# Three PSUM buffers for the exps of a scan kernel, products with C one scan later, and sums over states in bursts in a shared PSUM bank

## The chip, the core and the metric

The kernel runs on one core of one Trainium2 chip. The core has TensorE (PE, matrix products), VectorE (DVE), ScalarE (ACT, activation functions), GpSimd (POOL) and SyncE (SP, which here issues nearly all transfers). They run at once, each through its own queue in order, and wait for one another by semaphores. Matrix products land in PSUM, which has eight banks of 512 float32 columns on 128 partitions; everything else lies in SBUF. The metric is the device time of one execution in microseconds, the lower the better.

## The reference

Eight images of 56 x 56 pixels with 192 channels go through four layers: three state-space layers (the first with a convolution branch beside it) and one window-attention layer with an MLP. All is float32. The change touches the core of the state-space layers, the selective scan. For each of 4 directions k over the 3,136 pixels, each of 192 channels d and each of 16 states n:

```python
def step(h, t):
    u_t, d_t, b_t, c_t = t
    h = exp(d_t[..., None] * A) * h + (d_t * u_t)[..., None] * b_t[:, :, None, :]
    return (h, einsum('bkdn,bkn->bkd', h, c_t))
ys = scan(step, 0, (xs4, delta, Bs, Cs)) + Ds * xs4      # and a sum over the directions
```

Directions 0 and 2 run over rows forwards and backwards, 1 and 3 over columns. Delta is the softplus of a small projection; B and C are other rows of the same projection.

## The kernel before, in words

**Tiling.** A chunk is 784 pixels (CK), four per direction. A unit is one layer of one image, one direction and one chunk: 8 images x 3 layers x 4 x 4 = 384 units. A unit has two halves h of 96 channels. A half has 12 steps: three channel groups j of 32 channels times four state groups sg of 4 states. A tile of 128 partitions holds 32 channels x 4 states. That makes 9,216 steps; `run` writes them out in one order, and all engines follow it.

**A step.** In `make`, ScalarE computes exp(delta x A) from `dsp` (delta spread over four states, by a transfer) into a PSUM buffer `ps_x` of two banks, and GpSimd computes `db = usp x bt` (delta x u, spread likewise, times a row of B spread over 32 channels). VectorE then runs the scan over the 784 columns, in place in `ps_x`, with the last state of the chunk before as its start. It multiplies the result with `ct` (the row of C) into `hc`. Every fourth step the scan writes to `hc` and GpSimd does that product. ScalarE copies the scan's last column to `state` (all but the last chunk). TensorE multiplies `hc` with `esum`, a 128 x 32 matrix of ones and zeros, which adds the four states up, and accumulates in PSUM.

**The order in `run`, before.** At step s: the state copy of step s-2, then the exp and db of step s, then scan and product of step s-1 on VectorE, GpSimd's product of step s-2 if it has one, and the sums of three products (j = 0, 1, 2) up to step s-4. Within a half, sg is the outer loop and j the inner one. The sums of a half lie in a buffer of their own, `ps_y` (two banks), which begins with a product of the identity (or of D) with what is accumulated so far; at its end one copy (`merge`) of 96 x 784 brings it back to `act`. PSUM holds two buffers `ps_x` (four banks), `ps_y` (two) and two single banks `ps_p` for all other work.

**Other work.** Projections, softplus, layer norms, convolutions and attention of neighbouring images run beside the scans. They are Python generators in three queues (`ahead`, `urgent`, `back`). At the end of each step the loop lets them issue pieces while a budget for TensorE and ScalarE (SPARE, MOST, unchanged) lasts. `yield 1` puts a piece off to the next step; LAG = 1 is the distance between a matmul and what reads its bank. A piece takes a bank by `bank` or `all_banks` and gives it back with `free`. Functions that need another activation table (softplus, silu, gelu) run in steps that `table_time` allows: step modulo 4 equal to 1 or 2.

**Transfers.** `prepare` computes delta and du for the next half and issues their spreads (2,304 of `dsp`, 2,304 of `usp`); `load_bc` issues the rows of B and C for the next unit (1,536 each). All stand in SP's queue in the order of the program, each waiting there for its buffer.

The functions that the change touches, as they were before:

Of the kernel before, what the change touches and what calls it, by code (L numbers as in the profile page):

```python
# [36 lines left out]
HW = 56  # L37
# [7 lines left out]
N = 16  # L45
# [93 lines left out]
class Net:  # L139
    def __init__(self, ctx, tc, a, out):  # L140
# [19 lines left out]
        self.psum = ctx.enter_context(tc.tile_pool(name="psum", bufs=2, space=bass.MemoryType.PSUM))  # L160
        self.psum1 = ctx.enter_context(tc.tile_pool(name="psum1", bufs=1, space=bass.MemoryType.PSUM))
        for n in (1, 2, 4):
            setattr(self, f"s{n}", ctx.enter_context(tc.tile_pool(name=f"s{n}", bufs=n)))
        self.s6 = ctx.enter_context(tc.tile_pool(name="s6", bufs=HCS))
# [12 lines left out]
    def ps(self, tag, p=128, n=512):  # L177
        if tag == "y":
            t = self.psum1.tile([128, 1024], F32, name="ps_y")
        elif tag == "p":  # L180
            t = self.banks[0]
            self.banks.rotate()
        else:
            t = self.psum.tile([128, 1024], F32, name=f"ps_{tag}", tag=tag)
        return t[:p, :n]
# [185 lines left out]
    def bank(self, spare=0):  # L371


        (p,) = yield from self.all_banks(1, spare)
        return p

    def all_banks(self, n, spare=0):
        rank = self.rank
        while len(self.banks) < n + spare or any(at >= self.now - 1 for at in self.asked[rank + 1 :]):
            self.asked[rank] = self.now  # L380
            yield 1
        self.asked[rank] = -9
        return [self.banks.popleft() for _ in range(n)]

# [8 lines left out]
    def table_time(self):  # L393


        while self.step % 4 not in (1, 2) and not self.forced:
            yield 1
# [9 lines left out]
    def together(self, width, works):  # L407
# [3 lines left out]
        while works or tasks:  # L411
# [10 lines left out]
            else:  # L422
                yield 1
# [4 lines left out]
    def ln_cm(self, x, n, sq):  # L428
# [10 lines left out]
        yield 1  # L439
        yield from self.to_norm(x, n, sq)  # L440

    def to_norm(self, x, n, sq):
# [3 lines left out]
        yield 1  # L446
# [11 lines left out]
        yield 1  # L458
# [41 lines left out]
    def ssm_front(self, b):  # L500
# [3 lines left out]
        with tc.tile_pool(name="f1", bufs=1) as f1, tc.tile_pool(name="f2", bufs=2) as f2:  # L504
# [14 lines left out]
            def depthwise(r, c, u):  # L519
# [13 lines left out]
                yield 1  # L533

            def gate(xnt, r, e, sz):
# [12 lines left out]
                yield 1  # L548
# [3 lines left out]
            for r in range(NR + 1):  # L552
                sz = u = None
                if r < NR:
# [15 lines left out]
                    yield 1  # L570
# [3 lines left out]
                    yield 1  # L574
# [10 lines left out]
                    yield 1  # L585
# [7 lines left out]
                yield 1  # L593
# [8 lines left out]
    def conv_front(self, b):  # L602
# [3 lines left out]
        with tc.tile_pool(name="f1", bufs=1) as f1, tc.tile_pool(name="f2", bufs=2) as f2:  # L606
# [20 lines left out]
            def first(r):  # L627
# [15 lines left out]
                yield 1  # L643

            def second(r):
# [7 lines left out]
                yield 1  # L653

            def third(r):
# [6 lines left out]
                yield 1  # L662
# [3 lines left out]
                def last(c):  # L666
# [6 lines left out]
                    yield 1  # L673
# [10 lines left out]
                    yield 1  # L684
# [35 lines left out]
    def after_half(self, g, q):  # L720
# [6 lines left out]
        if l == 2:  # L727
            w = aux.rearrange("p c (a b) -> p c a b", b=HW)
            for c in range(2):
# [5 lines left out]
                yield 1  # L735
# [6 lines left out]
        yield 1  # L742
        if l == 0:
# [6 lines left out]
            ps = yield from self.all_banks(2)  # L750
            for c in range(2):
                for j in range(2):
                    nc.tensor.matmul(
                        ps[c][:CH, :HC], self.wout[:, j, CH * c : CH * c + CH], y[:, j, :],
# [775 lines left out]
```

## Time and profile before

| What | Value |
|---|---|
| Median of three runs | 27,059.5 us (27,051.76 to 27,069.66) |
| Span of the profiled execution, first to last instruction | 27,058.8 us; the page gives no other time of that execution |
| Instructions | 260,255 |
| Busy: TensorE, VectorE, ScalarE, GpSimd | 68%, 89%, 64%, 85% of the span |
| Granted TensorE clock, mean | 0.756 |
| DMA engines busy in the main queue | 56.0%; 128 GB/s |
| Scans, 128 x 784 | 9,216 of 1.78 to 1.85 us each |
| Products with C on VectorE, on GpSimd | 6,912 of 0.975 us, 2,304 of 1.847 us |
| Products db on GpSimd | 9,216 of 1.857 us |
| Exps on ScalarE | 9,216 of 0.919 us |

A group line of the profile names engine, operation, output and inputs by the program's names, shapes and count; behind the first bar stand the busy time in us and the mean of one in ns; behind the second the idle time of that engine just before these instructions, with what ended most of it. Nearly all instructions are recorded under one line of the program (L109, a helper), so groups are told apart by names and shapes. In a list of waits the numbers are us in total, how often, and the longest. In a timeline the first numbers are start and duration in us.

### The profile page before, as it was taken

What the parts mean: (1) busy time and instruction counts of PE and PEld (TensorE: products, weight loads), DVE (VectorE), ACT (ScalarE), POOL (GpSimd) and SP (SyncE); (2) the same over time, 40 slices, a digit from 0 to 9 for tenths busy, and PEclk for the clock granted to TensorE, in tenths of its full rate; (3) what the DMA queues carried; (4) which work ended last, traced back from release to release, by engine and by line L of the source; (5) the groups of instructions that cost most, each with busy time, mean ns of one, the idle gap of its engine ahead of it and who ended that gap; (6) DMA issues with size and microseconds to landing.
All of it is one profiled execution on the core that took longest, in us unless ns stands there. A gap on an engine that the chain in (4) does not pass through costs nothing. (4 is left out here: it accounts for less than half of the span.)

```text
span 27058.8 us, 260255 instructions
## 1 busy us (share of the span) xinstructions
PE 18495.3 (68%) x76788; PEld 6432.0 (24%) x76788; DVE 24122.4 (89%) x18972; ACT 17211.8 (64%) x30893; POOL 23054.4 (85%) x13199
## 2 busy tenths in 40 slices
PE   6675567676676666766667676677766776676657
PEld 2221122222222222222222222222212222222114
DVE  5999999999999899999999999989999899999991
ACT  4655566665666666666666666666666666666655
POOL 5888988888888888888888888888888888888991
PEclk7776677777777777777777777777777777777777
DMA  4555565556555565555655556555565555555550
GB/s 96 135 138 124 133 136 133 126 127 139 135 132 127 125 144 132 132 126 129 142 131 132 127 131 140 133 129 127 131 140 131 129 128 135 134 129 129 130 132 25
DMA packets 1503447, 3472.21 MB, mean 128 GB/s; under 512 B 310618, under 2 KB 503219, under 8 KB 1502020
## 3 DMA queue, kind: packets, MB, share of 16 engines
q1 hardware_dynamic: 1496452, 3455.15, 56.0%
q8 instruction: 606, 9.93, 0.1%
q0 software_dynamic: 3072, 0.31, 0.1%
q14 instruction: 821, 6.73, 0.1%
q10 hardware_dynamic: 2496, 0.09, 0.0%
HBM read 1457.23 MB, written 147.89 MB: 59 GB/s over the span
## 5 line engine op out<-in xcount | busy, mean ns | idle before, releaser
L109 POOL TENSOR_TENSOR db<-usp,bt 128x784 f32<-128x784 f32 x9216 | 16832.7, 1857 | 161.8 <-DMA usp<-du 129.3
L109 DVE TENSOR_TENSOR_SCAN ps_x<-ps_x,state,db 128x784 f32<-128x784 f32 x5184 | 9569.7, 1846 | 834.0 <-ACT state L109 358.7
L109 ACT ACTIVATE ps_x<-dsp,A 128x784 f32<-128x784 f32 x9216 | 8464.1, 919 | 2496.9 <-DVE hc L109 2190.5
L109 PE MATMUL ps_y<-hc,esum 128*32 128x392 f32 x36864 | 6959.3, 641 | 1147.3 <-POOL hc L109 780.6
L109 DVE TENSOR_TENSOR hc<-ps_x,ct 128x784 f32<-128x784 f32 x6912 | 6739.5, 975 | 651.4 <-DVE ps_x L109 11.0
L109 POOL TENSOR_TENSOR hc<-hc,ct 128x784 f32<-128x784 f32 x2304 | 4254.4, 1847 | 2696.2 <-ACT state L109 2104.5
L109 ACT COPY state<-ps_x 128x1 f32<-128x1 f32 x5184 | 831.4, 160 | 4659.5 <-DVE hc L109 4637.4
L109 DVE TENSOR_TENSOR_SCAN hc<-ps_x,state,db 128x784 f32<-128x784 f32 x1728 | 3181.7, 1841 | 161.6 <-POOL db L109 58.2
L109 DVE TENSOR_TENSOR_SCAN ps_x<-ps_x,db 128x784 f32<-128x784 f32 x1728 | 3085.0, 1785 | 261.1 <-ACT state L109 149.1
L109 PEld LDWEIGHTS ps_y<-hc,esum 128*32 128x32 f32 x36864 | 1630.6, 130 | 6096.7 <-issue 3212.3
L109 PE MATMUL ps_y<-act,ident 96*96 96x392 f32 x2304 | 1612.2, 835 | 1760.4 <-ACT act L109 1746.4
L109 PE MATMUL ps_p<-act,act 13*96 13x392 f32 (+1 forms) x3072 | 1513.0, 605 | 1116.6 <-ACT s L109 210.4
L109 POOL TENSOR_TENSOR du<-delta,act 96x784 f32<-96x784 f32 x768 | 1567.9, 2042 | 201.3 <-ACT delta L109 198.7
L109 PE MATMUL ps_p<-act,wx 96*88 96x392 f32 (+1 forms) x1536 | 985.8, 778 | 686.9 <-ACT delta L109 394.0
L109 ACT ACT_TABLE_LOAD x896 | 1149.6, 1283 | 34.4 <-PE ps_p L109 18.9
L390 ACT ACT_TABLE_LOAD x897 | 1150.9, 1283 | 15.6
L109 PEld LDWEIGHTS ps_y<-act,ident 96*96 96x96 f32 x2304 | 465.0, 223 | 2603.1 <-ACT act L109 2056.6
L109 DVE TENSOR_TENSOR_SCAN hc<-ps_x,db 128x784 f32<-128x784 f32 x576 | 1025.8, 1781 | 58.8 <-ACT state L109 38.0
L109 PEld LDWEIGHTS ps_p<-act,act 13*96 13x96 f32 (+1 forms) x3072 | 465.4, 180 | 2033.6 <-issue 373.5
L109 ACT COPY act<-ps_y 96x784 f32<-96x784 f32 x768 | 928.0, 1208 | 8.5 <-PE ps_y L109 8.5
L109 PE MATMUL ps_p<-xip,diag 96*96 96x448 f32 x2016 | 864.0, 580 | 94.4 <-ACT delta L109 94.3
L109 ACT COPY state<-hc 128x1 f32<-128x1 f32 x1728 | 328.6, 190 | 883.6 <-DVE hc L109 880.4
(212 smaller groups left out, 18126.0 us busy)
## 6 DMA issues: line engine op xcount, KB each, us to landing
dsp<-delta SPq DMA_DIRECT2D x2304, 392.0 KB
usp<-du SPq DMA_DIRECT2D x2304, 392.0 KB
bt<-bcd SPq DMA_DIRECT2D x1536, 392.0 KB
ct<-bcd SPq DMA_DIRECT2D x1536, 392.0 KB
wf<-in_wf SPq DMA_DIRECT2D x128, 288.0 KB
wf<-wf2d SPq DMA_DIRECT2D x128, 288.0 KB
bcd<-bcx SPq DMA_DIRECT2D x256, 134.8 KB
szd<-sz SPq DMA_DIRECT2D x56, 336.0 KB
```

The lines of the kernel that those rows point to most:

```text
L109: return call(out, *args, **k)
L390: self.tc.nc.scalar.preload_act_table_set(LN_EXP)
```

## The change

**PSUM.** `ps_x` has three buffers (six banks). `ps_y` is gone: the sums use one of the two single banks. The buffers in SBUF become rings of their own (RINGS): three `dsp` and `usp` in place of four, five `bt`, six `ct`, four `db`, seven `hc` in place of eight.

**Steps.** Within a half, j is now the outer loop and sg the inner one, so four steps in a row share `dsp` and `usp` and make up one group of 32 channels. At step s VectorE gets the scan of step s-1 and then the product of step s-2. The step whose product GpSimd makes is sg = 1 (AWAY), and it is issued at s-3.

**Sums.** A group's four products are added up in two bursts, the first at the end of the group's sixth step (`begin_sum`, then sg 0 and 2), the second one step later (sg 1 and 3), with the merge in that same step. The 784 columns are cut into three parts of 280, 280 and 224 (PARTS), which go to three 32-partition parts of one bank. The merge is three copies of 32 partitions per group, nine per half. `bank_now` takes the bank for it and lets waiting pieces run until one is free; `kept` makes other work leave one over.

**Other work.** It runs twice a step: once behind the exp and db and ahead of the scan, and once behind the product. Many `yield 1` become `yield NEAR` (0.5). Table switches come at step modulo 4 equal to 0, at most one task a step; `prepare` takes both banks only at step modulo 4 equal to 3.

**Transfers.** The spreads are put in a list (`later`) and issued nine steps before the group that uses them. The rows of B and C are loaded by `load_rows`, at four late steps of a unit, B one step ahead of C.

The core of the diff:

```diff
-        self.psum = ...tile_pool(name="psum", bufs=2, space=PSUM)
-        self.psum1 = ...tile_pool(name="psum1", bufs=1, space=PSUM)
+        self.psum = ...tile_pool(name="psum", bufs=3, space=PSUM)
...
     def table_time(self):
-        while self.step % 4 not in (1, 2) and not self.forced:
-            yield 1
+        while (self.step % SN or self.switched == self.step) and not self.forced:
+            yield NEAR
+        self.switched = self.step
...
             if s < S:
                 made[s] = self.make(*steps[s])
+            while self.later and self.later[0][0] <= s:
+                self.spread_rows(*self.later.popleft()[1:])
+            self.near = True
+            self.pieces(left)
             t = s - 1
             if 0 <= t < S:
-                U, h, sg, j = steps[t]
+                U, h, j, sg = steps[t]
                 x, db = made[t]
-                pool = t % 4 == 3
-                hc = self.s6.tile([128, CK], F32, name="hc")
-                hs = hc if pool else x
+                hs = x
+                if sg == AWAY:
+                    hs = products[t] = self.ring("hc")
                 nc.vector.tensor_tensor_scan(hs[:, sense], x[:, sense], db[:, sense], ...)
-                if not pool:
-                    nc.vector.tensor_mul(hc, hs, self.C_[U, sg])
                 made[t] = hs
             t = s - 2
-            if 0 <= t < S and t % 4 == 3:
-                nc.gpsimd.tensor_mul(weighed[t], weighed[t], self.C_[U, sg])
-            t = s - 4
-            if 0 <= t < S and t % 3 == 2:
-                self.add_up(U, h, sg, [weighed.pop(t - 2 + d) for d in range(3)])
-                if sg == NSG - 1:
-                    copies.append((s + 2, U, h))
-            if copies and copies[0][0] <= s:
-                self.merge(*copies.popleft()[1:])
+            if 0 <= t < S:
+                hs = made.pop(t)
+                if sg != AWAY:
+                    products[t] = self.ring("hc")
+                    nc.vector.tensor_mul(products[t], hs, self.C_[U, sg])
+            t = s - 3
+            if 0 <= t < S and steps[t][3] == AWAY:
+                nc.gpsimd.tensor_mul(products[t], products[t], self.C_[steps[t][0], AWAY])
+            t = s - SN - 2
+            if 0 <= t < S and t % SN == 0:
+                for sg in LATE:
+                    self.add_up(self.sums, products.pop(t + sg), sg == LATE[-1])
+            self.near = False
+            self.now += NEAR
+            self.pieces(left)
+            if 0 <= t < S and t % SN == 0:
+                self.merge(*steps[t][:3], self.sums)
+                self.free(self.sums)
+            t = s - SN - 1
+            if 0 <= t < S and t % SN == 0:
+                self.sums = self.bank_now()
+                self.begin_sum(*steps[t][:3], self.sums)
+                for sg in EARLY:
+                    self.add_up(self.sums, products.pop(t + sg), False)
...
+    def begin_sum(self, U, h, j, p):
+        w, t = (self.dd[:, h, :], u) if U.begins else (self.ident[:CH, :CH], y)
+        for q, (at, n) in enumerate(PARTS):
+            self.nc.tensor.matmul(p[G * q : G * q + G, :n], w[:, G * j : G * j + G],
+                view(t, k, h, i * CK + at, n), start=True, stop=False)
+    def add_up(self, p, hc, stop):
+        for q, (at, n) in enumerate(PARTS):
+            self.nc.tensor.matmul(
+                p[G * q : G * q + G, :n], self.esum, hc[:, at : at + n], start=False, stop=stop)
+    def merge(self, U, h, j, p):
+        for q, (at, n) in enumerate(PARTS):
+            self.nc.scalar.copy(
+                view(y, k, h, i * CK + at, n), like(p[G * q : G * q + G, :n], k))
...
-LAG = 1
-HCS = 8
+LAG, NEAR = 1, 0.5
+RINGS = (("dsp", 3), ("usp", 3), ("bt", 5), ("ct", 6), ("db", 4), ("hc", 7))
+PARTS = ((0, 5 * HW), (5 * HW, 5 * HW), (10 * HW, 4 * HW))
+AWAY = 1
+EARLY, LATE = (0, 2), (AWAY, 3)
+LOADS = (("bt", 1), ("ct", 2))
```

One small part lies outside the scans: the output projection of the first layer takes its two banks one after the other, and writes its first half by way of `aux`, with a copy of 96 x 392 on ScalarE behind it (64 in all).

## The prediction

> **What bounds the kernel now.** I read the busy times first, then the groups of VectorE, then a timeline of VectorE where nothing disturbs it, then who ends its waits. The page's line of busy times:
>
> ```profile
> PE 18495.3 (68%) x76788; PEld 6432.0 (24%) x76788; DVE 24122.4 (89%) x18972; ACT 17211.8 (64%) x30893; POOL 23054.4 (85%) x13199
> ```
>
> VectorE is the fullest engine and GpSimd is close behind. The stages differ, so I cut the span at the first and the last scan; the columns after the colon are stretch, then busy time with instruction count of PE, PEld, DVE, ACT, POOL:
>
> ```profile
> 181.00:26410.60 26229.60, 17967.35 (x73560) 6136.34 (x73560) 24036.95 (x18748) 16800.26 (x29821) 22935.79 (x13047) 0.76 0.58 131
> 26410.60:27058.80 648.20, 462.49 (x3096) 270.95 (x3096) 76.56 (x168) 357.84 (x967) 54.01 (x65) 0.77 0.10 26
> ```
>
> The scans fill 26,230 us (9,216 steps, 2.85 us each); 181 us before them and 648 us after them (the last image's attention) have no scan. In the new program the instructions behind the last exp are the same in kind and number to within two, so these 829 us stay. Inside, VectorE idles 2,192 us. The groups (busy, mean ns, then idle before it and what ended that):
>
> ```profile
> L109 DVE TENSOR_TENSOR_SCAN ps_x<-ps_x,state,db 128x784 f32<-128x784 f32 x5184 | 9569.7, 1846 | 834.0 <-ACT state L109 358.7 <-ACT ps_x L109 300.8 <-POOL db L109 130.6
> L109 DVE TENSOR_TENSOR hc<-ps_x,ct 128x784 f32<-128x784 f32 x6912 | 6739.5, 975 | 651.4 <-DVE ps_x L109 11.0 <-PE ps_p L109 2.7 <-issue 1.8
> ```
>
> The products lose 651 us, 94 ns each, to no other engine: each waits for the scan just ahead of it. An undisturbed stretch of VectorE shows it (start, duration):
>
> ```profile
> 26379.64 1.83 DVE L109 TENSOR_TENSOR_SCAN ps_x<-ps_x,state,db 128x784 f32<-128x784 f32 x1
> 26381.58 0.98 DVE L109 TENSOR_TENSOR hc<-ps_x,ct 128x784 f32<-128x784 f32 x1
> 26382.47 1.85 DVE L109 TENSOR_TENSOR_SCAN ps_x<-ps_x,state,db 128x784 f32<-128x784 f32 x1
> ...
> 26388.16 1.84 DVE L109 TENSOR_TENSOR_SCAN hc<-ps_x,state,db 128x784 f32<-128x784 f32 x1
> 26389.92 1.83 DVE L109 TENSOR_TENSOR_SCAN ps_x<-ps_x,state,db 128x784 f32<-128x784 f32 x1
> ```
>
> A product starts 1.95 us after its scan (1.85 long); the scan behind a product starts 0.89 us after it (0.97 long), and a scan behind an unrelated scan 1.76 us after it. So unrelated neighbours overlap by 0.08 us, and a scan with its own product leaves a gap of 0.10. Last, the waits of VectorE within the scans:
>
> ```profile
> DVE ps_x L109 <- ACT state L109: 507.8, 301, 42.8
> DVE ps_x L109 <- ACT ps_x L109: 358.0, 243, 10.9
> DVE ps_x L109 <- POOL db L109: 174.8, 66, 26.0
> DVE hc L109 <- ACT state L109: 91.0, 51, 3.0
> DVE hc L109 <- POOL db L109: 76.6, 89, 7.2
> DVE hc L109 <- ACT ps_x L109: 44.9, 42, 2.7
> ```
>
> ScalarE ends 1,002 us of them (its exps come late behind other work), GpSimd 251.
>
> **Products one scan later: −1,270 us.** The same 6,912 products remain, and now follow the scan of the next step. If they then follow it like any unrelated instruction, a product starts 1.755 us after it and not 1.95: 5,184 × 0.195 = 1,011 us. For first chunks (scans of 1.78) the steps are 1.85 and 1.70: 1,728 × 0.15 = 259. A rule speaks against this: the Trainium skill, "VectorE: DVE Perf Modes", section "The DRAIN you can't avoid", says that the pipe is emptied behind every instruction and that a semaphore between two of them costs nothing extra; by that the gain is 0. The same page lets an instruction that isn't held start earlier, and the rows above show 1.76 against 1.95, so I take the rows. Ends: 0 and −1,270. A product now also waits for the state copy of its step on ScalarE, since both read one PSUM tile (now the copy waits for the product: it starts 0.03 us after its end). The copy lies ahead of the next exp, which the scan behind this product needs anyway, so I add nothing; that scan is what would be late.
>
> **ScalarE: third exp buffer and more copies: +300 us.** By the deferral an exp's buffer comes free one scan later, so the third buffer only restores the lead of now; I give it no gain. The one copy of sums per half (768) becomes 9 of 32 partitions. Two stretches of the trace show the cost of the old one:
>
> ```profile
> L109 ACT COPY act<-ps_y x73: 801/807/1627, 11020.5 to 13495.0; 96x784 f32<-96x784 f32 x73
> L109 ACT COPY act<-ps_y x148: 801/1602/1639, 615.4 to 5578.0; 96x784 f32<-96x784 f32 x148
> ```
>
> 0.80 us in rows, 1.60 in columns (strided). With a fixed 0.16 (the 128x1 state copy) and the rest by length, copies of 280, 280 and 224 take 0.39+0.39+0.34 = 1.12 or 0.68+0.68+0.57 = 1.93: mean 1.53 × 2,304 groups = 3,520 us against 928. ScalarE goes from 17,212 to some 19,860 us with 64 added 96x392 copies. What it costs depends on where it falls. From each program's order I summed ScalarE's work between one exp and the next at the row durations (state copy left out). Mean by step modulo 4: now 0.33, 2.02, 0.56, 0.58 us; changed 1.80, 0.36, 1.94, 0.53. The room is the time of two scans less two exps with their hand-overs (2.46 us, from the timeline): 3.2 us now (2.1 next to the scan without a product), 3.0 and 2.1 then. Work above the room sums to 922 us now, which agrees with the 1,002 measured, and to 1,143 to 1,604 changed (with the 0.08 overlap of neighbouring copies and the state copy out of the way, or without both). So +220 to +680; I take 300, near the lower end, because that one counts the overlaps that the rows show. Most is the softplus with two table loads (2 × 1.28 + 0.9 us) and the merge in steps 4m+2.
>
> **Other work twice a step: +350 us.** What is issued in the first half of a step now stands ahead of a scan on VectorE, but behind the new exp on ScalarE. In the new order 195 of the 526 norm chains (Ln and Exp on ScalarE, then a product on VectorE) lie wholly in a first half; before, all stood behind a scan, and these waits come to 30 us (17.5 for act, 12.2 for ao). VectorE then waits for the exp and Ln and Exp: 0.13 + 0.92 + 0.54 + 0.47, some 2.0 us with hand-over, with the scan and the product queued behind: 195 × 2.0 = 390. A tenth falls where ScalarE is late anyway: 350 (0 to 410; 0 if exps run well ahead, against which their buffers speak).
>
> **GpSimd: +150 us.** It does the same 9,216 + 2,304 + 768 products, 22,936 us within the scans, and so gets fuller as steps get shorter. Its product with C waits one step less tightly, but du has one buffer, and its last spread is now issued only one step before the half starts, with du of the next half two steps later: that one waits for the transfer, with db behind it, and the scans wait for db. I add 150 to the 251 us; ends −100 (the looser product) and +500 (0.65 us per half).
>
> **Transfers: −50 us.** Their number and size stay. The spreads are issued nine steps ahead of use, after three to four now; waits of db and exps for them are 129 and 109 us in the groups, mostly hidden. The rows of B have some four steps (10 us), and stand on SP behind spreads that wait for exps. Ends −150 and +150.
>
> **Sums: +50 us.** PE streams the same 784 columns per product, as three parts in three column groups (now two parts, three products abreast; 12 records took 1.52 to 2.84 us). But they borrow one of two shared banks for about one step in four, and the merge stands in the same step as the last sums. Behind those sums on PE is other work; behind the merge is the exp. Ends 0 and +400.
>
> **Sum.** −1,270 + 300 + 350 + 150 − 50 + 50 = −470. The profiled span is 27,058.8 us, the median of the runs 27,059.5, so 0.7 lies between: 26,589, say **26,590 us**.
>
> **Rivals.** *More of the gain stays* (0.2): if ScalarE's lateness and the chains fall together, the two terms give 200 in place of 650, and the product of GpSimd's looseness offsets the 150: 27,059 − 1,270 + 200 = about 25,990. The quiet tail of VectorE speaks for it; the two engines at 85 to 90% against. *ScalarE's merge waits for PE* (0.25), the one on the other side: in steps 4m+2 the merge takes 1.12 to 1.93 us of 2.1 us of room. The last sums wait for a product that ends as this exp starts; if PE then comes 0.5 us too late for the room in the mean, with its other work or a borrowed bank ahead of the sums, every group's next scan slips: 2,304 × 0.5 = 1,152, or 27,740 us. It decides from 0.2 us per group (470 / 2,304). PE's 68% and its clock of 0.76 speak for it, the sums' age of two steps against. *The gap stays* (0.1): products behind a foreign scan start no earlier, while the costs come in part: 27,050 with the gain cut to half and costs to 630. 0.45 is left for the forecast, whose own range is 26,250 to 26,950.
>
> **Chances and range.** Differences below 0.2% (54 us) are about what a measurement can't tell from no change. Faster is the forecast, the first rival and a fifth of the third: 0.67; same 0.07, from the third; slower 0.26. The range 25,900 to 27,450 leaves out about 0.08 below (costs near their lower ends) and 0.1 above (the merge's wait near 0.4 us or more).
>
> **What would show it.** Right: products with an idle time near 0 and 1.75 us behind a scan; scan waits on ScalarE of 1,200 to 1,600 us; act, ao, proj and qk products waiting some 350 us for ps_p; ScalarE at 19,800 us. Wrong: a gap of 0.1 us ahead of products again, db ending more than 700 us of waits, or ScalarE idle ahead of the copies to act with PE as its cause.

## The result, and the profile after

The changed kernel takes 29,990.6 us in the median (29,969.3 to 30,000.4) and the kernel before 27,062.0 us (27,051.8 to 27,069.7), four executions each: the ratio is 1.108, with a 95% interval of 1.1065 to 1.1096. The change costs 2,929 us. The profiled execution has a span of 29,967.5 us. The page's line of busy times:

```profile
PE 20068.8 (67%) x105972; PEld 8673.4 (29%) x105972; DVE 23554.2 (79%) x18972; ACT 19332.9 (65%) x37101; POOL 23091.8 (77%) x13199
```

VectorE does its 18,972 instructions in 568 us less than before, and ScalarE has 2,121 us more to do. But VectorE was to stay the bound, and it is busy 79% of the span now: its idle time went from 27,058.8 − 24,122.4 = 2,936 us to 29,967.5 − 23,554.2 = 6,413 us. Between the two profiled executions the loss is 2,909 us: 3,477 us of new idle time less the 568 us. It lies within the scans; the stretch behind the last of them has its old length (stretch, then busy time with count of PE, PEld, DVE, ACT, POOL, clock, DMA share, GB/s):

```profile
181.00:29317.00 29136.00, 19539.30 (x102738) 8376.59 (x102738) 23458.14 (x18741) 18923.69 (x36026) 22968.47 (x13044) 0.72 0.52 118
29317.00:29967.50 650.50, 466.85 (x3111) 273.01 (x3106) 80.65 (x172) 357.01 (x969) 52.13 (x64) 0.76 0.10 26
```

Five of the groups show where VectorE idles (busy, mean ns, then idle before it and what ended that), and that ScalarE's copies of sums now wait too:

```profile
L109 DVE TENSOR_TENSOR_SCAN ps_x<-ps_x,state,db 128x784 f32<-128x784 f32 x5184 | 9518.5, 1846 | 2694.5 <-POOL db L109 1321.4 <-issue 855.6 <-ACT ps_x L109 502.9
L109 DVE TENSOR_TENSOR hc<-ps_x,ct 128x784 f32<-128x784 f32 x6912 | 6597.1, 954 | 533.4 <-ACT state L109 519.1
L109 ACT COPY act<-ps_p 32x280 f32<-32x280 f32 x4608 | 2416.7, 524 | 3907.8 <-PE ps_p L109 3873.4
L109 ACT COPY act<-ps_p 32x224 f32<-32x224 f32 x2304 | 1039.9, 451 | 29.8
L109 POOL TENSOR_TENSOR du<-delta,act 96x784 f32<-96x784 f32 x768 | 1571.0, 2046 | 2087.4 <-DMA usp<-du 853.9 <-ACT delta L109 456.8 <-ACT ps_x L109 421.0
```

The first group idled 834 us before. The copies take 2,416.7 + 1,039.9 = 3,457 us, 1.50 us per group of 32 channels. The list of waits (us, times, longest) puts the forms together by the tile that is written; `hc` there is written by products and by the scans that GpSimd's product follows. Seven of its rows:

```profile
ACT act L109 <- PE ps_p L109: 3873.4, 1974, 9.1
DVE ps_x L109 <- POOL db L109: 1777.6, 687, 19.4
DVE ps_x L109 <- issue: 1251.7, 486, 10.1
POOL du L109 <- DMA usp<-du: 853.9, 229, 11.1
DVE ps_x L109 <- ACT ps_x L109: 612.8, 299, 13.5
DVE hc L109 <- ACT state L109: 519.1, 600, 39.0
DVE act L109 <- ACT ps_p L109: 383.5, 149, 6.9
```

"Issue" is a wait for which the profile shows no releaser. An undisturbed stretch of the timeline shows the deferral at work (start, duration):

```profile
13028.83 1.78 DVE L109 TENSOR_TENSOR_SCAN ps_x<-ps_x,db 128x784 f32<-128x784 f32 x1
...
13030.52 0.95 DVE L109 TENSOR_TENSOR hc<-ps_x,ct 128x784 f32<-128x784 f32 x1
...
13031.40 1.77 DVE L109 TENSOR_TENSOR_SCAN hc<-ps_x,db 128x784 f32<-128x784 f32 x1
```

A product starts 1.69 us after a scan of 1.78: the gap of 0.10 is gone and neighbours overlap. Those are scans of a first chunk. For later chunks, to which the prediction's 1.95 belongs, another stretch has two pairs:

```profile
14025.09 1.86 DVE L109 TENSOR_TENSOR_SCAN ps_x<-ps_x,state,db 128x784 f32<-128x784 f32 x1 [5.38 <-POOL db L109]
14026.85 0.96 DVE L109 TENSOR_TENSOR hc<-ps_x,ct 128x784 f32<-128x784 f32 x1
...
14035.69 1.85 DVE L109 TENSOR_TENSOR_SCAN ps_x<-ps_x,state,db 128x784 f32<-128x784 f32 x1
14037.88 0.97 DVE L109 TENSOR_TENSOR hc<-ps_x,ct 128x784 f32<-128x784 f32 x1 [0.34 <-ACT state L109]
```

The first product starts 1.76 us after its neighbour, as predicted. The second had to wait 0.34 us for ScalarE's state copy and starts 2.19 us after it. A third stretch shows what the change was paid with:

```profile
13006.33 2.25 POOL L109 TENSOR_TENSOR du<-delta,act 96x784 f32<-96x784 f32 x1 [3.36 <-DMA usp<-du]
...
13008.54 5.48 POOL L109 TENSOR_TENSOR db<-usp,bt 128x784 f32<-128x784 f32 x3
...
13010.42 1.80 DVE L109 TENSOR_TENSOR_SCAN ps_x<-ps_x,db 128x784 f32<-128x784 f32 x1 [2.33 <-POOL db L109]
13011.58 1.92 ACT L109 COPY act<-ps_p 32x280 f32<-32x280 f32 x3 [5.11 <-PE ps_p L109]
...
13013.62 0.91 ACT L109 ACTIVATE ps_x<-dsp,A 128x784 f32<-128x784 f32 x1
...
13014.62 1.80 DVE L109 TENSOR_TENSOR_SCAN ps_x<-ps_x,db 128x784 f32<-128x784 f32 x1 [2.40 <-ACT ps_x L109]
```

GpSimd's du waits 3.36 us for a spread out of its only buffer, the db behind it is late, and the scan waits 2.33 us. ScalarE waits 5.11 us for TensorE at the head of the copies of sums, with the next exp behind them, and the scan of that exp waits 2.40 us. The experiments price these waits.

### The profile page after: what moved, and what is told of

It is laid out like the page before. It is cut to its first block, busy times and chain, and to the rows that moved or that the text cites. A ratio compares the mean times of both kernels' runs of the same rounds, so it can differ in the third digit from the quotient of the medians.

```text
span 29967.5 us, 323390 instructions
## 1 busy us (share of the span) xinstructions
PE 20068.8 (67%) x105972; PEld 8673.4 (29%) x105972; DVE 23554.2 (79%) x18972; ACT 19332.9 (65%) x37101; POOL 23091.8 (77%) x13199
## 5 line engine op out<-in xcount | busy, mean ns | idle before, releaser
L109 PE MATMUL ps_p<-hc,esum 128*32 128x280 f32 (+1 forms) x55296 | 7634.4, 518 | 2366.7 <-DVE hc L109 2263.1
L109 DVE TENSOR_TENSOR hc<-ps_x,ct 128x784 f32<-128x784 f32 x6912 | 6597.1, 954 | 533.4 <-ACT state L109 519.1
L109 ACT COPY act<-ps_p 32x280 f32<-32x280 f32 (+1 forms) x6912 | 3456.6, 500 | 3937.6 <-PE ps_p L109 3873.4
L109 PEld LDWEIGHTS ps_p<-hc,esum 128*32 128x32 f32 x55296 | 3826.8, 142 | 5773.5 <-DVE hc L109 3174.3
L109 POOL TENSOR_TENSOR du<-delta,act 96x784 f32<-96x784 f32 x768 | 1571.0, 2046 | 2087.4 <-DMA usp<-du 853.9
L109 PE MATMUL ps_p<-act,ident 96*32 96x280 f32 (+1 forms) x10368 | 2168.9, 631 | 1166.3 <-ACT delta L109 758.3
L109 PE MATMUL ps_p<-act,act 13*96 13x392 f32 (+1 forms) x3072 | 1841.8, 699 | 581.5 <-ACT act L109 480.3
L109 PEld LDWEIGHTS ps_p<-act,ident 96*32 96x32 f32 x10368 | 385.2, 131 | 2560.1 <-ACT delta L109 1049.2
L109 PE MATMUL ps_p<-xb,wf 96*128 96x392 f32 x1392 | 758.6, 693 | 318.2 <-POOL xb L109 104.0
```

Of the source, the lines that this page charges most:

```text
L109: return call(out, *args, **k)
```

## The experiments

Theory at the start: the deferral works, and three misplacements with the added ScalarE work cost more than it brings: the merge in the same step as the last sums (the rival on the other side), the one du buffer, the first half of the step. Rivals: the deferral itself is the loss, or the two shared banks. Each edit is a single execution beside one of the kernel before, which took 27,057 to 27,074 us. Unless said otherwise, differences are to the changed kernel at 29,991.

### The deferral taken back in the changed kernel

```diff
+            made.pop(t, None)
             if s < S:
                 made[s] = self.make(*steps[s])
...
                 made[t] = hs
+                if sg != AWAY:
+                    products[t] = self.ring("hc")
+                    nc.vector.tensor_mul(products[t], hs, self.C_[U, sg])
-            t = s - 2
-            if 0 <= t < S:
-                U, h, j, sg = steps[t]
-                hs = made.pop(t)
-                if sg != AWAY:
-                    products[t] = self.ring("hc")
-                    nc.vector.tensor_mul(products[t], hs, self.C_[U, sg])
```

> The changed kernel with the product moved back directly behind its own scan; all else as changed, so the exps now have a third buffer and a real lead of one scan more. If the deferral does what the prediction says, the gap of 0.10 us comes back (6,912 x 0.19 = about 1,270 us of VectorE) and products idle some 640 us for their scan. If the time is lost in waits on GpSimd and ScalarE (theory), the longer steps fill part of these waits and the extra lead of the exps helps: 29,600 to 30,400 us. If the deferral itself causes the loss (rival: products now wait for state copies on ScalarE, 519 us, and hold exp buffers), the time falls well below 29,000 us.

Measured: 30,365 us, +375. The group of products has its old idle time back:

```profile
L109 DVE TENSOR_TENSOR hc<-ps_x,ct 128x784 f32<-128x784 f32 x6912 | 6738.9, 975 | 676.9 <-DMA ct<-bcd 37.4 <-DVE ps_x L109 15.5 <-PE ps_p L109 7.2
```

So the deferral isn't the loss, but taking it back costs only 375 us, not 1,270.

### Two buffers for du

```diff
-        du = self.s1.tile([CH, CK], F32, name="du")
+        du = self.s2.tile([CH, CK], F32, name="du")
-RINGS = (... ("hc", 7))
+RINGS = (... ("hc", 6))
```

> The changed kernel with two buffers for du in place of one, paid for by six buffers hc in place of seven. Theory: GpSimd's du stands behind the last spread of the old du, which stands on SP behind a spread of delta that waits for an exp; its 2,087 us of idle time ahead of du make db late (scans wait 1,912 us for db). Then du waits under 900 us, scans wait under 1,000 us for db, and the time falls by 700 to 1,500 us, to 28,500 to 29,300 us. Rival: du waits as long for softplus on ScalarE, and something else is late: less than 300 us fall, 29,700 us or more.

Measured: 29,371 us, −620, one hc buffer less included. That is a little under the 700 expected. The wait of du for its spreads is gone (the one for softplus is 659 us, 457 before the edit), and scans into `ps_x` wait 740 us for db in place of 1,778. Their "issue" wait grows from 1,252 to 1,499, so part of the lateness shows elsewhere.

### Other work in one place, behind scan and product

```diff
-            self.near = True
-            self.pieces(left)
             t = s - 1
...
             self.near = False
             self.now += NEAR
             self.pieces(left)
+            self.pieces(left)
```

> The changed kernel with both passes of other work behind scan and product of the step (no first half ahead of the scan); the half steps of their clock stay. The prediction gave the first half 350 us. Products of norm chains waited 735 us in all for ScalarE in the changed kernel's groups (384 act, 177 ao, 64 proj, 59 kn, 51 qk) and matmul readers 500 us for TensorE. Theory: these waits go back to under 250 us together, and the time falls by 700 to 1,200 us, to 28,750 to 29,250 us. Rival (they only fill time in which GpSimd or ScalarE would be waited for): under 300 us.

Measured: 29,400 us, −591, also under the 700 expected. The products of the norm chains (act, ao, proj, kn, qk) wait 610 us for ScalarE in place of 735, act far less and qk and kn more: 125 us together. The rest is other work too, of kinds that the prediction didn't count. First the changed kernel, then this one:

```profile
L109 DVE RECIPROCAL sm<-sm 128x6 f32<-128x6 f32 x256 | 47.2, 184 | 238.6 <-ACT s L109 130.7 <-ACT state L109 107.2 <-POOL s L109 0.8
L109 DVE TENSOR_SCALAR ps_p<-ps_p 96x392 f32<-96x392 f32 x232 | 130.8, 564 | 256.7 <-PE ps_p L109 256.3
```

```profile
L109 DVE RECIPROCAL sm<-sm 128x6 f32<-128x6 f32 x256 | 45.9, 179 | 40.6 <-ACT s L109 39.5 <-POOL s L109 0.4
L109 DVE TENSOR_SCALAR ps_p<-ps_p 96x392 f32<-96x392 f32 x232 | 126.6, 557 | 102.6 <-PE ps_p L109 102.4
```

These two fall by 352 us. Over all of VectorE's groups, its idle time ahead of other work falls by 658 us and ahead of products by 98; ahead of scans it grows by 153. The merge's wait for TensorE falls by 640 us, to 3,233, but the scans gain nothing by it.

### The merge one step later

The merge stands behind the exp and db of the next step:

```diff
             if s < S:
                 made[s] = self.make(*steps[s])
+            t = s - SN - 3
+            if 0 <= t < S and t % SN == 0:
+                self.merge(*steps[t][:3], self.sums)
+                self.free(self.sums)
...
-            t = s - SN - 2
-            if 0 <= t < S and t % SN == 0:
-                self.merge(*steps[t][:3], self.sums)
-                self.free(self.sums)
```

> The changed kernel with the three copies of a group moved from the step of the last sums to behind the exp of the next step; the bank is held half a step longer. ScalarE idles 3,873 us at these copies for TensorE, with an exp behind them. If that is a main cause (the second rival of the prediction), the idle time falls under 1,500 us, scans wait less for exps and the time falls by 800 us or more, below 29,200 us. If ScalarE only waits there in place of waiting for an exp's buffer a moment later, it falls by less than 300 us.

Measured: 28,782 us, −1,209, or 0.52 us per group. Its waits:

```profile
ACT act L109 <- PE ps_p L109: 2036.9, 975, 9.0
DVE hc L109 <- ACT state L109: 1619.9, 1112, 39.1
DVE ps_x L109 <- POOL db L109: 1024.6, 515, 19.5
```

The merge waits 1,836 us less. Of the scans into `ps_x`, the "issue" waits go from 1,252 to under 50 us, the waits for exps from 613 to 179, and those for db from 1,778 to 1,025. The edit takes two things out of the next exp's way at once: ScalarE's wait for sums that TensorE hasn't finished, and the three copies themselves, 1.50 us per group. How the 1,209 us divide between them isn't shown. Products now wait 1,620 us for the state copies, where 519 stood.

### The state copies behind the product as well

```diff
-            t = s - 2
-            if 0 <= t < S and not steps[t][0].last:
-                U, h, j, sg = steps[t]
-                end = CK - 1 if U.k < 2 else 0
-                nc.scalar.copy(self.at_state(h, j, sg), made[t][:, end : end + 1])
+            for t in (s - 3, s - 2):
+                if 0 <= t < S and (steps[t][3] == AWAY) == (t == s - 2):
+                    ...   # the same copy
```

> The kernel with the merge behind the next exp, and the state copies of the three products of VectorE issued one step later, behind the product and ahead of the next exp (as in the kernel before). With the merge moved, products idle 1,620 us for state copies that now stand behind merge and other work. Theory: with the copy behind the product that wait is gone (products under 100 us), part of it comes back as waits for exps: 400 to 1,000 us less than 28,782, so 27,800 to 28,400 us. Rival: ScalarE is late in itself and the scans wait for the exps in its place: within 250 us of 28,782.

Measured: 29,352 us, +570 to the kernel with the late merge. The wait of products is 0, and scans wait in its stead:

```profile
L109 DVE TENSOR_TENSOR hc<-ps_x,ct 128x784 f32<-128x784 f32 x6912 | 6592.1, 954 | 0.0
L109 DVE TENSOR_TENSOR_SCAN ps_x<-ps_x,state,db 128x784 f32<-128x784 f32 x5184 | 9466.0, 1846 | 1602.6 <-POOL db L109 882.3 <-ACT ps_x L109 451.3 <-ACT state L109 211.3
L109 DVE TENSOR_TENSOR_SCAN hc<-ps_x,state,db 128x784 f32<-128x784 f32 x1728 | 3185.4, 1843 | 943.8 <-issue 579.2 <-POOL db L109 186.6 <-POOL du L109 108.6
```

So this place for the copies is no remedy. The edit also keeps each exp buffer busy until its later copy, so it doesn't tell whether ScalarE is late in itself or the exps now wait for buffers.

### The three repairs together, then all four

Late merge, two du buffers and one place, by the diffs above:

> Merge behind the next exp, two buffers du (six hc), and both passes of other work behind scan and product, together; state copies as changed. If the three causes are apart, their gains add: 29,991 - 1,209 - 620 - 591 = 27,570 us. If they are one lateness seen in three places, the sum is not reached: 28,200 us or more.

Measured: 27,407 us, −2,584, a little more than the single gains add up to (1,209 + 620 + 591 = 2,420). By what was expected, these are costs apart from one another, and not one lateness seen in three places. It is the fastest version of the change that computes everything, and still 333 us (1.2%) slower than the kernel before beside it.

```profile
DVE hc L109 <- ACT state L109: 1511.1, 1199, 41.3
ACT act L109 <- PE ps_p L109: 1468.3, 888, 7.6
POOL du L109 <- ACT delta L109: 1032.8, 410, 101.3
DVE ps_x L109 <- POOL db L109: 500.1, 232, 19.0
```

With the later state copies on top:

> The same with the late state copies as well. If the deferral and the third exp buffer are worth what the prediction says (about 1,270 us) and the loss lies in these four places, it comes near or under the kernel before: 26,700 to 27,500 us. If GpSimd, ScalarE and the two shared banks still make it late: 27,800 us or more.

Measured: 27,609 us, +202, between the two expectations. Products idle 10 us in place of 1,535, scans 2,570 in place of 995: as before, the wait moves.

### The kernel before with the copies of the sums in six pieces

```diff
-                    copies.append((s + 2, U, h))
+                    copies.extend([(s + 1, U, h, 0), (s + 2, U, h, 1), (s + 2, U, h, 2)])
...
-        self.nc.scalar.copy(dst, p)
+        y = self.bufs[(U.g + 1) % 2][G * j : G * j + G]
+        for q in range(2):
+            self.nc.scalar.copy(
+                view(y, k, h, i * CK + q * HC, HC), like(U.sums[h][G * j : G * j + G, q, :], k))
```

> The kernel before with its one copy of sums per half as six copies of 32 x 392, two in one step and four in the next (by the rows 2.9 us per half in place of 0.80, or 5.3 in place of 1.60): 2,250 us more of ScalarE, near the 2,590 of the changed kernel, but far behind the sums they read. If ScalarE's added work is what costs, 700 us or more; if it is where the copies stand (theory: the copy right behind its sums makes ScalarE wait for TensorE), 0 to 400 us: 27,070 to 27,470 us.

Measured: 27,932 us, +859 to the kernel before beside it, for 1,755 us more on ScalarE (18,967 against 17,212). A third of the copies stands one step earlier than the one copy did, but they hardly wait for TensorE here; the scans wait for ScalarE:

```profile
DVE ps_x L109 <- ACT state L109: 854.7, 450, 42.5
DVE ps_x L109 <- ACT ps_x L109: 587.8, 364, 7.1
ACT act L109 <- PE ps_y L109: 72.4, 88, 8.5
```

Those two waits were 508 and 358 us. ScalarE is two thirds busy, and in this place 0.49 us of each added microsecond lands on the end.

### Two parts in place of three; du two steps behind its softplus

In the repaired kernel, the 784 columns as two parts, which makes six copies per half out of nine:

```diff
-PARTS = ((0, 5 * HW), (5 * HW, 5 * HW), (10 * HW, 4 * HW))
+PARTS = ((0, HC), (HC, HC))
```

> The kernel of merge, du and place together (27,407 us), with the 784 columns of the sums in two parts of 392 in place of three: six copies per half of 0.48 or 0.89 us for nine, some 370 us less of ScalarE (2,304 x 0.16) and a third fewer matmuls. If ScalarE's added copies are what is left of the loss (the six copies in the kernel before cost 859 us for 1,755 us of ScalarE, 0.49 of it), 150 to 350 us less: 27,050 to 27,260 us. Rival: the wait of the merge for TensorE (1,468 us) is what counts, and two column groups make the sums longer: 27,400 us or more.

Measured: 28,134 us, +727 to the repaired kernel, although ScalarE has 343 us less to do and TensorE's clock was granted at 0.80 (0.75 there). Two timelines, of this kernel and of the repaired one, show the sums in a burst that nothing interrupts (a run of matmuls is drawn together; each product and part leaves two records, so both lines are four products):

```profile
13028.11 2.81 PE L109 MATMUL ps_p<-hc,esum 128*32 128x392 f32 x16
```

```profile
13017.12 2.27 PE L109 MATMUL ps_p<-hc,esum 128*32 128x224 f32 x24
```

The same four products take 2.81 us in two column groups and 2.27 in three. The merge's wait for TensorE grows from 1,468 to 2,652 us and the products' wait for state copies from 1,511 to 2,059. The reading that fits is that the length of the sums on TensorE counts through ScalarE, even with the merge a step later; the copies are longer here too (0.68 us each), which isn't tested apart. ScalarE's busy time is not what counts by itself: it has less to do, and its state copies come later.

On top of it, `yield 2` for `yield 1` behind the softplus, so that du is issued a step later:

> Two parts as well, and du issued two steps behind the softplus in place of one. GpSimd waits 1,033 us ahead of du for the softplus, with db behind it, and scans wait 606 us for db. If that is still paid for: 150 to 450 us less than with two parts alone. If GpSimd's lead covers it: within 100 us of it.

Measured: 28,170 us, +36. GpSimd's wait for softplus halves (1,257 to 556 us) and nothing comes of it; that wait was covered.

### The deferral taken back in the repaired kernel

The first diff, in the repaired kernel:

> The kernel of merge, du and place together, with the product back behind its own scan. In the changed kernel that cost 375 us only, where VectorE was 79% busy. The prediction's step says 1,270 us where VectorE is the bound. If less of VectorE's time is covered by other waits here (86% busy), it is worth more than 375: 27,900 to 28,700 us. If the deferral's own waits for state copies (1,511 us here) eat it, 27,400 us or less.

Measured: 27,695 us, +288, neither of the two expectations. The products:

```profile
L109 DVE TENSOR_TENSOR hc<-ps_x,ct 128x784 f32<-128x784 f32 x6912 | 6736.1, 975 | 1029.2 <-PE ps_p L109 232.6 <-DMA ct<-bcd 125.5 <-DVE ps_x L109 12.8
```

They idle 1,029 us against 1,535 with the deferral: there the wait for state copies (1,511 us, and none here) more than takes the place of the gap. With the deferral VectorE is 665 us less busy and idles 216 us less ahead of scans; the products' 506 us and 87 us at other work take part of that away.

### Four shared banks and two exp buffers

```diff
-        self.banks = deque(... for n in range(2))
+        self.banks = deque(... for n in range(4))
-        self.psum = ...tile_pool(name="psum", bufs=3, space=PSUM)
+        self.psum = ...tile_pool(name="psum", bufs=2, space=PSUM)
```

With two exp buffers the product has to follow its own scan, so the comparison is the kernel with the deferral taken back.

> The changed kernel with two exp buffers in place of three and the product behind its own scan (as in the kernel before), and four shared banks in place of two; sums, merge, loops, transfers and halves of a step as changed. Beside the kernel with own scan and three buffers (30,365 us) it has two more banks and one exp buffer less. If the shared bank is the root (the sums stand on TensorE behind other work that waits for a bank, and the merge behind the sums), ScalarE waits under 2,000 us at the merge in place of 3,901, and the time is 28,500 to 29,600 us. If the merge's place alone matters, whatever the banks: 30,000 us or more.

Measured: 30,452 us against 30,365. The merge's wait for TensorE falls from 3,901 to 1,611 us, but scans into `ps_x` wait 2,132 us for db (1,619), and those into `hc` 189 us for exps (104). In the repaired kernel:

> The same with merge behind the next exp, two du (six hc) and other work in one place. With three buffers, two banks and its own scan this was 27,695 us. If banks still cost there (the merge waits 1,417 us for TensorE): 26,900 to 27,400 us. If the third exp buffer is worth as much: 27,500 us or more.

Measured: 27,922 us against 27,695. The merge's wait falls here too, from 1,417 to 627 us. Two further banks for one exp buffer lose 87 us, hardly more than executions of one kernel differ, and 227. The gains that were expected if the banks are the root didn't come. But each edit takes a buffer away as it gives the banks, so what the banks alone are worth stays untested.

### A third of the merge copies, with and without the deferral

In the repaired kernel, of each group's three copies only the first. The kernel then leaves out bringing back the sums of 504 of the 784 columns; their buffer is set to zero once at the start:

```diff
-        for q, (at, n) in enumerate(PARTS):
+        for q, (at, n) in enumerate(PARTS[:1]):
             self.nc.scalar.copy(
```

> The repaired kernel (merge later, two du buffers, one place; 27,407 us), but of the three merge copies of a group only the first, 280 of the 784 columns, is made: the accumulated sums of the other 504 columns are left out, so the output is not the reference's (the buffer is set to zero once at the start). ScalarE loses 1,536 + 3,072 copies, some 2,300 us, and stands near 16,900, below the kernel before. Theory (the added ScalarE work is what remains of the loss): the scans' and products' waits for ScalarE fall, and the time goes below the kernel before, to 26,300 to 26,800 us, because the deferral's 290 us then stay. If what remains is the order of the steps (spreads, state copies, other work) and not the length of the copies: 27,100 us or more, and the products still wait over 1,200 us for state copies.

Measured: 26,727 us, −680 to the repaired kernel and 332 below the kernel before beside it. ScalarE's busy time falls by 2,248 us, to 17,096, about what it was before the change:

```profile
PE 18976.7 (71%) x105972; PEld 8450.7 (32%) x105972; DVE 23485.6 (88%) x18972; ACT 17096.1 (64%) x32493; POOL 23091.4 (86%) x13200
```

With the product directly behind its scan again:

> The repaired kernel with a third of the merge copies (26,727 us), and the product again directly behind its own scan; as there, the sums of 504 of 784 columns are not brought back, so the output is not the reference's. If the deferral's gain is small only because ScalarE is late (its state copies hold the product up), it must be worth more where ScalarE has 2,240 us less to do: 27,150 us or more, a difference of over 420. If the gain is 290 to 375 us whatever ScalarE has to do: 27,020 to 27,100 us. The products' wait for state copies, 933 us with the deferral, should be under 250 here in either case.

Measured: 27,217 us, so the deferral is worth 490 us here, and the copies that are left out 478 us without it (27,695 to 27,217, for 2,210 us of ScalarE). The products of the two, first with the deferral and then without:

```profile
L109 DVE TENSOR_TENSOR hc<-ps_x,ct 128x784 f32<-128x784 f32 x6912 | 6611.9, 957 | 938.8 <-ACT state L109 932.7 <-PE ps_p L109 3.4
```

```profile
L109 DVE TENSOR_TENSOR hc<-ps_x,ct 128x784 f32<-128x784 f32 x6912 | 6739.2, 975 | 1009.3 <-PE ps_p L109 194.7 <-DMA ct<-bcd 143.8 <-DVE ps_x L109 16.9
```

In the repaired kernel the gain grows from 288 to 490 us as ScalarE's work and the products' wait for state copies (1,511 to 933 us) fall; the shared bank comes free sooner there too, which isn't tested apart. The wait alone doesn't give the size: 1,270 less the wait that comes with the deferral is 751, −241 and 337 us in the three pairs, where 375, 288 and 490 were measured. What the pairs have in common is VectorE's busy time, which the deferral makes 628, 665 and 634 us shorter. The other half of the 1,270, the gap, isn't gained: products idle 144 us less with the deferral in the changed kernel, 506 more in the repaired one and 71 less here.

### The deferral alone, in the kernel before

To defer without a third exp buffer, every scan writes to its buffer in SBUF, and the product follows one scan later, in place:

```diff
-                hs = hc if pool else x
+                hs = hc
...
-                if not pool:
-                    nc.vector.tensor_mul(hc, hs, self.C_[U, sg])
...
-            if 0 <= t < S and t % 4 == 3:
+            if 0 <= t < S:
                 U, h, sg, j = steps[t]
-                nc.gpsimd.tensor_mul(weighed[t], weighed[t], self.C_[U, sg])
+                (nc.gpsimd if t % 4 == 3 else nc.vector).tensor_mul(
+                    weighed[t], weighed[t], self.C_[U, sg])
```

> The kernel before with the deferral alone: every scan writes into its buffer in SBUF, and the product with C follows one scan later, in place. No third exp buffer, no other change; nothing is left out of the computation. If the deferral is worth what the changed kernel showed (290 to 375 us): 26,680 to 26,800 us. If it is worth the 1,270 us of the prediction where nothing else changes: 25,800. If a product that reads and writes SBUF is slowed by GpSimd's traffic, or a product that waits for the state copy (both now touch one SBUF tile, and the product overwrites what the copy reads) costs more than the bubble: 27,100 or more; then products take over 1.0 us each, or end over 600 us of waits on ScalarE.

Measured: 31,684 us, +4,625 to the kernel before. Products on VectorE take 1.80 us in the mean where 0.975 stood, and GpSimd's db 2.21 where 1.857 stood:

```profile
L109 DVE TENSOR_TENSOR hc<-hc,ct 128x784 f32<-128x784 f32 x6912 | 12465.7, 1803 | 730.1 <-ACT state L109 717.7 <-DMA ct<-bcd 6.5 <-DMA bt<-bcd 1.2
L109 POOL TENSOR_TENSOR db<-usp,bt 128x784 f32<-128x784 f32 x9216 | 20171.3, 2214 | 405.4 <-DVE hc L109 356.1 <-DMA usp<-du 30.6 <-DMA bt<-bcd 14.4
```

The timeline shows that the two engines hardly work side by side:

```profile
13012.41 1.84 POOL L109 TENSOR_TENSOR db<-usp,bt 128x784 f32<-128x784 f32 x1
13012.76 2.31 DVE L109 TENSOR_TENSOR hc<-hc,ct 128x784 f32<-128x784 f32 x1 [0.29 <-ACT state L109]
13014.20 2.58 POOL L109 TENSOR_TENSOR du<-delta,act 96x784 f32<-96x784 f32 x1
```

VectorE's product is issued 0.35 us into GpSimd's db and ends 0.82 us after it, so it hardly ran beside it; the du behind it takes 2.58 us, where the kernel before has 2.04. The Trainium skill, "SBUF — State Buffer", section "SBUF: two separate sides", has a rule for it: the two engines share one pair of ports, which a VectorE instruction with two SBUF inputs or a GpSimd instruction, whichever starts first, takes for its whole length, and the other is blocked. The trace agrees: of the product's 0.975 us, 0.82 lie behind the end of db. Without a third exp buffer, in this form, the deferral loses; what it is worth alone in the kernel before stays open.

## Why the prediction was wrong

The forecast was 26,590 us, with a range to 27,450; the kernel takes 29,991. Every step that was measured was off in size, and one wait was put at nothing. By the steps of the prediction:

- **Products one scan later (−1,270 us).** Products do start earlier behind a foreign scan, 1.76 us after it as reckoned, and the gain of 0 that the rule on the emptied pipe gave is excluded. The step that failed is the sentence on the state copy, "so I add nothing". The product's wait for it is 519 us in the changed kernel and 1,511 in the repaired one, none with the product behind its own scan. About half of the forecast gain, VectorE's shorter busy time, came each time; the gap's half didn't, and 375, 288 and 490 us are left. The wait grows when ScalarE waits longer for TensorE (two parts) and falls when it has less to copy (a third of the copies), which fits a late ScalarE; why the gain is larger in the changed kernel than in the repaired one is open.
- **ScalarE: third buffer and more copies (+300 us).** The copies' length was right (1.53 us per group predicted, 1.50 measured); ScalarE as a whole has 19,333 us, 527 less than said. The price was too low: 680 us for two thirds of the copies in the repaired kernel with the deferral, 478 without it, 859 us for 1,755 us of copies in the kernel before. That is 0.30, 0.22 and 0.49 us per added microsecond, where 300 us for some 2,650 is 0.11. Counting only what exceeds the room between two exps took ScalarE to be on time with everything else.
- **Other work twice a step (+350 us).** 591 us when taken back alone. The mechanism was right, and the count was short: it priced the norm chains, which gave 125 us, and left out VectorE's other instructions that read what ScalarE or TensorE has only just been asked for (in the softmax, the clamp of the norms, the convolutions).
- **GpSimd (+150 us, at most 500).** The mechanism was seen, down to the transfer that du waits for, and under-sized: 620 us. The upper end was reckoned as 0.65 us per half. The wait of du for spreads is 1.1 us per half in the mean, and comes in pieces of 3.7 us (853.9 us in 229 waits) with the db of the next steps behind it. A sign of being wrong that the prediction gave, db ending more than 700 us of waits, came true with 1,912.
- **Sums in the shared bank (+50 us, at most 400).** This is the largest miss: 1,209 us for the merge's place in the step of the last sums. The prediction had this place as a rival at 1,152 us and gave it a quarter. Measured is 0.52 us per group against the rival's 0.5; that 0.5 was assumed and not worked out, and the 1,209 also hold the copies' own length ahead of the exp, so the closeness is luck. The place was named rightly: ScalarE idle ahead of the copies to act with TensorE as its cause was the sign, and it is the longest line of ScalarE's waits.
- **Transfers (−50 us).** Not measured apart. Besides those of du, the rows of B came late: db waits 427 us for them in the changed kernel and 384 in the repaired one, where 19 stood. No run takes that back.

VectorE's idle time, summed over its groups, shows the steps side by side (us):

| Kernel | ahead of scans | ahead of products with C | ahead of other work |
|---|---|---|---|
| before | 1,316 | 651 | 910 |
| changed | 3,873 | 533 | 1,948 |
| one place | 4,026 | 436 | 1,290 |
| late merge | 1,504 | 1,636 | 2,091 |
| three repairs | 995 | 1,535 | 1,333 |
| a third of the copies | 1,041 | 939 | 1,200 |

The three misplacements together make 2,584 us of the 2,929, shown by taking them back in one kernel. What keeps that kernel behind the kernel before is in the table: products wait for state copies, and other work still idles 423 us more than before, with its half steps (`NEAR`) not taken back. Leaving out two thirds of the merge copies brings 680 us, more than the 345 that remain, and takes some of both.

The range failed on sizes first: with the gain as measured and every cost at its upper end, the sum is 27,059 − 375 + (680 + 410 + 500 + 150 + 400) = 28,824 us. And it took the rival's price as an alternative to the other costs, where the costs add up. TensorE's clock was granted at 0.72 in the changed kernel, 0.756 before and 0.751 with the three repairs; whether the lower clock is a cause of the late sums or goes with the longer time isn't shown.

## What to carry to other kernels

An engine that waits in order passes its lateness on to whatever stands behind the waiting instruction, so place an instruction that waits for another engine behind the work that the bound engine needs next, and let what feeds it be a step old. When work moves ahead of the bound engine's next instruction, count every instruction of it that waits there, not one kind. A bubble taken from the bound engine is only worth what its feeders can follow: before pricing it, ask what each of them must deliver per step, and price added work on a feeder that is two thirds busy at a good part of its length (0.22 to 0.49 of it here), not at the excess over an average room. Where a rival names a place and a price from the program's order, such as a wait in the same step as its source, count it into the sum with its chance, beside the other costs.

## What the runs showed of the hardware

- A VectorE product with two SBUF operands beside GpSimd products takes 1.80 us in the mean against 0.975 with one operand in PSUM, and GpSimd's take 2.21 against 1.857: 4,625 us in this kernel.
- Three column groups of TensorE with 32 columns each take four products of 784 columns in 2.27 us, two groups in 2.81 us, at a higher granted clock over the run (0.80 against 0.75).
- A higher granted clock didn't go with a shorter time: 28,134 us at 0.80, 27,407 at 0.75.
- Without a dependence a product starts 1.76 us behind a scan of 1.86 us, before its end; behind its own scan of 1.85 us it starts 1.95 us after the start.
